# A graph attention layer: 40 instead of 32 columns per group copied by ScalarE, with one of two id loads moved ahead

## The chip, the core and the metric

The kernel runs on one core of a Trainium2 chip. The metric is the device time of one execution in microseconds; lower is better. The core has five engines with queues of their own: TensorE (PE in the profile, its weight loads PEld), VectorE (DVE), ScalarE (ACT), GpSimd (POOL) and the sync engine (SP), which issues most of the transfers. An engine's queue is handed out in order by its sequencer; instructions of the sequencer itself (loads of registers, register arithmetic) carry a q in the profile (ACTq).

## The reference

One layer of attention over a graph with N = 12500 nodes, 212500 edges sorted by target node, width 128 and 8 heads of 16. Everything is 32-bit float.

```python
Q, K, V = x @ WQ, x @ WK, x @ WV            # per node, reshaped (N, 8, 16)
Eh = edge_attr @ WE                          # per edge
score = K[src] * Q[dst] / sqrt(16) * Eh
score = exp(clip(score.sum(-1, keepdims=True), -5, 5))
wV = segment_sum(V[src] * score, dst)        # per target node
Z  = segment_sum(score, dst)
h  = x + wV / (Z + 1e-6)
h  = batchnorm(h) * gamma + beta             # over the nodes
out = layernorm(x + h)                       # over the width
```

## The kernel before

The edges lie in 1661 tiles of 128 edges. A group `g` is 8 tiles (two windows of 4), and there are 208 groups. First the kernel writes a table `kvd` of K and V for all nodes to memory (one row of 256 numbers a node). Then the main loop runs over the groups. For each tile of a group, K and V of the 128 source nodes must be brought into a slot in the on-chip memory. That is done in three ways:

- **By GpSimd.** `load_kv` appends one indirect transfer per tile (`gather`, line 272) to a list `queued`, as soon as a slot is free. A slot holds one group; the slot that `message(g)` frees is filled for group g+9. Groups 0 to 7 take another way and read no slot from `kvd`.
- **By ScalarE, as columns.** For the groups in `col_tiles` the last tile is left out of the gathers (`sizes[g] - (g in apart)`). Its 128 nodes are copied one column at a time out of `hx`, the transposed x that lies on the chip, into a tile `xc` (`fetch_cols`, line 363). Two matmuls with `w_kv` then give K and V (`cols_mm`, line 371, in the bank `ps_m`), and ScalarE copies them into the slot (`cols_out`, line 375). `COLS` is 32: 16 copies stand ahead of the exponentials of a group (`clip_exp`, lines 772 and 773) and 16 behind, so four groups make one tile. The column numbers are register values that ScalarE loads from `col_ids` (`load_cols`, line 326), in two loads of 16 words a group.
- **By the sync engine, as rows.** For the groups in `row_tiles` 16 rows a group come straight from `kvd` (`fetch_rows`, line 343), and ScalarE copies the full tile into the slot (`rows_out`, line 353).

The order on ScalarE in one group is: the first half of the column copies, the two exponentials (which wait for the scores `s` of VectorE), the second half of the copies, the writes of new x into a ring (`x_out`), `qs`, `os`, a column tile's K and V if one is due, two long copies `wt<-ps_e` (`eh_out`, line 715), the window of x for a later group (`q_window`, lines 654 and 661, `xw<-hx`; a load of 4 words from `base_i` in every second group), and the loads of the column numbers for the next group.

On VectorE a group is: `products` (line 755, which needs the gathered slot), `scores` (762), the clip (771), the work for later groups (684, 732, 809), `message` (777, which needs the exponentials) and `onehot` (674 to 677).

The order of all this is the order of the calls in the loop; nothing reorders it. From group 12 on the gathers are in addition paced: each is tied to a step of VectorE or TensorE in the loop.

Of the kernel before, what the change touches and what calls it, by code (L numbers as in the profile page):

```python
# [8 lines left out]
F32 = mybir.dt.float32  # L9
# [3 lines left out]
AF = mybir.ActivationFunctionType  # L13
OP = mybir.AluOpType
AX = mybir.AxisListType
ET = mybir.EngineType

P = 128
# [15 lines left out]
RING = 1024  # L34
MARGIN = 64
PAD = 2 * MARGIN + WN
COLS = 32
LOAD = 16
FIRST_COL = 8
COL_LAG = 2  # L40
SP_ROWS = 16
# [33 lines left out]
def col_plan(sizes):  # L75
    full = sizes.count(U) // 2
    groups, end = [], P
    while FIRST_COL + -(-end // COLS) - 1 + COL_LAG < full:
        groups.append(max(NX, FIRST_COL + -(-end // COLS) - 1 + COL_LAG))
        end += P  # L80
    assert sorted(set(groups)) == groups
    return groups


def row_plan(sizes):
    full, used = sizes.count(U) // 2, set(col_plan(sizes))
    groups, end = [], P
    while True:
        g = FIRST_ROW + -(-end // SP_ROWS) + ROW_LAG
        while g in used:  # L90
            g += 1
        if g >= full:
            return groups
        used.add(g)
        groups.append(g)
        end += P
# [7 lines left out]
def gnn_kernel(  # L104
# [19 lines left out]
    nc = tc.nc  # L124
    N, D = out.shape
# [19 lines left out]
    late = []  # L145
# [45 lines left out]
    hx = consts.tile([P, N + P], F32, name="hx")  # L191
# [66 lines left out]
    def slot(i):  # L258
        return rows.tile([P, 2 * G * P], F32, name=f"slot{i}")

    first = slot(NSLOT).rearrange("p (h c d) -> p h c d", h=2, d=2 * P)
# [34 lines left out]

    col_tiles = col_plan(usizes)
    tot = len(col_tiles) * P
    assert tot % (2 * COLS) == 0 and tot // (2 * COLS) <= P and P % COLS == COLS % LOAD == 0
    col_ids = consts.tile([P, 2 * COLS], I32, name="col_ids")  # L300
    row_tiles = row_plan(usizes)
    tot_rows = len(row_tiles) * P
# [6 lines left out]
    BY_ROW = {}  # L309
    XC = {}  # L310

    def load_col_ids():
        n, m = 2 * SP_ROWS, tot_rows // (2 * SP_ROWS)
        nc.sync.dma_start(row_ids[:m], bass.AP(tensor=rsrc.tensor, offset=rsrc.offset + tot, ap=[[n, m], [1, n]]))
        m = tot // (2 * COLS)
        nc.sync.dma_start(col_ids[:m], bass.AP(tensor=rsrc.tensor, offset=rsrc.offset, ap=[[2 * COLS, m], [1, 2 * COLS]]))

    OFFS = {}

    def load_cols(g):  # L320
        q = g - FIRST_COL
        if 0 <= q < tot // COLS:
            OFFS[g] = []
            for c in range(0, COLS, LOAD):
                at = q % 2 * COLS + c
                _, offs = nc.values_load_multi_w_load_instructions(
                    col_ids[q // 2:q // 2 + 1, at:at + LOAD], engines=(ET.Activation,), min_val=0, max_val=N - 1,
                    skip_runtime_bounds_check_because="node ids")
                OFFS[g] += offs

    def fetch_rows(g):
        q = g - FIRST_ROW
        if not 0 <= q < tot_rows // SP_ROWS:
            return
        c = q % 2 * SP_ROWS
        _, offs = nc.values_load_multi_w_load_instructions(
            row_ids[q // 2:q // 2 + 1, c:c + SP_ROWS], engines=(ET.SP,), min_val=0,
            max_val=(N - 1) * 8 * P, skip_runtime_bounds_check_because="node ids")
        for r, off in enumerate(offs, q * SP_ROWS):
            k = r // P  # L340
            if r % P == 0:
                BY_ROW[k] = late[0].tile([P, 2 * P], F32, name="byrow", bufs=2)
            d = nc.sync.dma_start(BY_ROW[k][r % P:r % P + 1, :].bitcast(U8), kvb[ds(off, 8 * P)].unsqueeze(0))
            d.then_inc(rows_in[k % NSEM], 16)
            tc.no_tile_sem_insts.add(d.ins.name)
            tc.add_to_no_dep_group(f"rows{k}", d.ins)

    def rows_out(g):
        k = (g - FIRST_ROW - ROW_LAG + 1) * SP_ROWS // P - 1
        if 0 <= k < len(row_tiles) and g == FIRST_ROW + -(-P * (k + 1) // SP_ROWS) - 1 + ROW_LAG:  # L350
# [1 line left out]
            tc.declare_fence(w.ins, group=f"rows{k}")  # L352
            step = nc.scalar.activation(KV[row_tiles[k]](G - 1, G, 0, 2 * P)[:, 0, :], BY_ROW[k], AF.Copy)
            tc.declare_no_dep(step.ins, group=f"rows{k}", reason="the semaphore of the rows")

    def fetch_cols(g, half):
        if g in OFFS:
            at = (g - FIRST_COL) * COLS
            for c in range(half * COLS // 2, (half + 1) * COLS // 2):
                k, r = col_tiles[(at + c) // P], (at + c) % P  # L360
                if r == 0:
                    XC[k] = late[0].tile([P, P], F32, name="xc", bufs=2)
                nc.scalar.activation(XC[k][:, r:r + 1], hx[:, ds(OFFS[g][c], 1)], AF.Copy)  # L363

    def col_tile(g):
        q = (g - FIRST_COL) * COLS
        return col_tiles[q // P - 1] if q > 0 and q % P == 0 and q <= tot else None

    def cols_mm(g):
        if col_tile(g) is not None:  # L370
# [62 lines left out]
    def within(f, g):  # L433
        return f(g) if 0 <= g < NG else None
# [99 lines left out]
    def load_quad(q):  # L534
        t = late[0].tile([P, RQ, U * P], U8, name="rbq", bufs=2)
        for h in (0, 1):
            nc.sync.dma_start(t[h * WN:(h + 1) * WN].rearrange("p a b -> p (a b)"), places(h, RQ * q, RQ))
        for k in range(RQ):
            RB[RQ * q + k] = t[:, k, :]
# [94 lines left out]
    def load(i):  # L634
        gs = range(2 * i, min(2 * i + 2, NG))
        if not gs:
            return
        t, n = wp.tile([P, 2, G, P], F32, name="ea", bufs=2), sum(nt(g) for g in gs)
        assert nt(2 * i) == G or len(gs) == 1
        for k, g in enumerate(gs):  # L640
            EA[g] = t[:, k]
        nc.sync.dma_start(t.rearrange("p c a b -> p (c a b)")[:, :n * P],
                          eaT[:, starts[2 * i] * P:(starts[2 * i] + n) * P])
# [249 lines left out]
    for q in range(NQ):  # L893
# [13 lines left out]
        k = q - first_step  # L907
# [64 lines left out]
    for g in range(NG - 2):  # L972
        if g % 2 == 0:
            load(g // 2 + 2)
        within(load_rel, g + 3)
        if (g + 6) % RQ == 0 and (g + 6) // RQ in quads:
            load_quad((g + 6) // RQ)
        fetch_rows(g)
        within(products, g)
        within(denom, g - 2)  # L980
        within(scores, g)
        fetch_cols(g, 0)
        within(clip_exp, g)
        within(recip, g - 2)
        within(turned_onehot, g + 2)
        within(both_halves, g + 1)
        late_x = g + 1 < nxg and g + 1 not in SLOT
        if late_x:
            turn_x(g + 1, 0, True)
            turn_x(g + 1, 4, True)  # L990
        within(add_x, g - 3)
        within(q_mm, g + 3)
        paced = g >= LATE + 4
        if not paced:
            issue()
        else:
            issue(G)
            for step in (SENT[g - 1], PARTS[g][1], PARTS[g][2], BY["both", g + 1]):
                pace(step)
        within(gather_sum, g - 1)  # L1000
        if paced:
            pace(BY["sum", g - 1])
        if not late_x:
            within(eh_mm, g + 2)
        cols_mm(g)
        fetch_cols(g, 1)
        within(x_out, g - 3)
        within(q_out, g + 3)
        within(sums_out, g - 1)
        cols_out(g)  # L1010
        rows_out(g)
        if late_x:
            project_main(g + 1)
            within(eh_mm, g + 2)
        within(eh_out, g + 2)
        within(q_window, g + 4)
        load_cols(g + 1)
        if paced:
            pace(BY["eh", min(g + 2, NG - 1)])
        within(turn_back, g + 1)  # L1020
        if paced:
            pace(BY["back", g + 1])
        within(qe_mm, g + 2)
        if paced:
            pace(BY["qe", min(g + 2, NG - 1)])
        within(attn, g - 2)
        within(message, g)
        within(onehot, g + 1)
        if g == 2:
            load_last()  # L1030
            nc.vector.tensor_scalar(row_ids, row_ids, 8 * P, None, op0=OP.mult)
        if g % (RUN // 2) == 2 and g > 2 and (g // (RUN // 2) + 1) * SEC < T:
            load_section(g // (RUN // 2) + 1)
        for i, r in enumerate(runs):
            if i and g == placed[i]:
                place(r)
        within_checks(g)
        while free and todo and todo[0] in done and not pending:
            load_x()
        bn_parts(2 * g - 5, 2 * g - 3)  # L1040
        if g == NG - 5:
            assert done >= set(range(NPRE))
            norm_first()
        if g == LATE - 1:
            tps.close()
            late.append(tps.enter_context(tc.tile_pool(name="late", bufs=1)))
        if g == LATE - 2:
            free.append(NSLOT)
            load_kv()
    last = NG - 1  # L1050
    g = last - 1
# [3 lines left out]
                           skip_runtime_bounds_check_because="a count")]  # L1055
# [332 lines left out]
```

## Time and profile before

| | us |
|---|---|
| median of 3 runs | 2059.93 (2055.01 to 2061.22) |
| the profiled execution, its own time | 2061.55 |
| its span, first to last instruction | 2059.6 |

| engine | busy us | share of the span | instructions |
|---|---|---|---|
| PE | 1768.6 | 86% | 9096 |
| DVE | 1543.5 | 75% | 3157 |
| POOL | 1541.2 | 75% | 1624 |
| ACT | 1225.2 | 59% | 8700 |

The chain that ended last lies in the last 60 us and tells nothing of the main loop. So the stage that counts must be read from the waits, the groups of instructions and the timeline. A row of a group reads: line, engine, operation, output<-inputs, shape, count | busy us, mean ns of one | idle us of the engine just before, and what ended it. A row of waits reads: who <- for whom: us in total, times, longest us. A row of the timeline reads: start us, us, engine, line, operation, names, count [idle before <- what ended it].

### The profile page before, as it was taken

Reading aid. Unit: us, or ns where it says so; the run is one execution under the profiler, and the core shown is the slowest. Engines: PE = TensorE matmul, PEld = TensorE weight load, DVE = VectorE, ACT = ScalarE, POOL = GpSimd, SP = SyncE. Lnnn points to the kernel's source line nnn. Section 1 sums busy time; section 2 is a strip of 40 time slices with the busy share of each in tenths; the row PEclk is TensorE's granted clock in tenths of the full one; section 3 lists DMA queues with packets and bytes.
Section 4 is the critical chain, followed back from the end, with each engine's and each line's share of the span. In section 5 each row is a group of like instructions: output and inputs, shape, how many; then the busy total and the mean of one; then the engine's idle time right before and its main releaser. Section 6 shows DMA issues by size and latency. Waiting matters only on the chain. (4 is left out here: it accounts for less than half of the span.)

```text
span 2059.6 us, 50464 instructions
## 1 busy us (share of the span) xinstructions
PE 1768.6 (86%) x9096; PEld 1121.2 (54%) x9096; DVE 1543.5 (75%) x3157; ACT 1225.2 (59%) x8700; POOL 1541.2 (75%) x1624
## 2 busy tenths in 40 slices
PE   7899999998888888888888888788888878888887
PEld 7676566665554545554554554454555445445556
DVE  4568899987777687777777777677777777777777
ACT  2356677766565565565665666565566566566545
POOL 7677777777777777777777777777777777777775
PEclk9999999999999999999999999999899999999998
DMA  7855556655555555555555555555555555555563
GB/s 266 304 184 180 190 186 195 203 182 188 180 167 185 174 178 175 174 188 170 175 187 166 175 190 161 181 186 175 167 184 174 170 179 184 164 179 184 192 202 127
DMA packets 133493, 379.50 MB, mean 184 GB/s; under 512 B 37631, under 2 KB 50602, under 8 KB 119338
## 3 DMA queue, kind: packets, MB, share of 16 engines
q0 software_dynamic: 75200, 204.05, 32.9%
q1 hardware_dynamic: 54776, 171.01, 23.7%
q14 instruction: 257, 2.11, 0.3%
q10 hardware_dynamic: 3186, 1.13, 0.2%
q8 instruction: 74, 1.21, 0.2%
HBM read 350.60 MB, written 25.44 MB: 183 GB/s over the span
## 5 line engine op out<-in xcount | busy, mean ns | idle before, releaser
L272 POOL DMA_INDIRECT slot<-kvd,srcs x1524 | 1451.5, 952 | 468.5 <-issue 283.5
L363 ACT ACTIVATE xc<-hx 128x1 f32 x6272 | 647.0, 190 | 267.5 <-issue 231.7
L755 DVE TENSOR_TENSOR slot<-slot,ps_t 128x512 f32<-128x512 f32 x410 | 271.4, 680 | 342.6 <-DMA slot<-kvd,srcs 254.8
L793 PE MATMUL ps_a<-msg,oh 128*128 128x136 f32 (+1 forms) x3322 | 519.6, 295 | 2.6 <-DVE msg L777 2.6
L793 PEld LDWEIGHTS ps_a<-msg,oh 128*128 128x128 f32 (+1 forms) x3322 | 419.3, 168 | 81.4 <-issue 52.2
L707 PE MATMUL ps_e<-ea,w_e 128*128 128x512 f32 x832 | 391.0, 592 | 0.1
L740 PE MATMUL ps_t<-ident,wt 128*128 128x128 f32 x1661 | 256.6, 295 | 125.0 <-DVE wt L732 121.6
L740 PEld LDWEIGHTS ps_t<-ident,wt 128*128 128x128 f32 x1661 | 197.7, 149 | 264.0 <-DVE wt L732 221.5
L777 DVE TENSOR_TENSOR msg<-slot,ps_m 128x1024 f32<-128x1024 f32 (+2 forms) x209 | 248.7, 1192 | 65.6 <-ACT slot L375 63.7
L772 ACT ACTIVATE ps_m<-s 128x64 f32<-128x64 f32 (+1 forms) x209 | 47.0, 225 | 399.1 <-DVE s L771 320.3
L732 DVE TENSOR_TENSOR wt<-wt,ps_q 128x512 f32<-128x512 f32 x416 | 264.6, 676 | 2.4 <-PE ps_q L722 2.3
L722 PE MATMUL ps_q<-ot,qs 64*128 64x512 f32 x832 | 264.3, 715 | 0.0
L762 DVE TENSOR_REDUCE s<-slot 128x64 f32<-128x1024 f32 (+1 forms) x208 | 249.8, 1202 | 0.2
L715 ACT ACTIVATE wt<-ps_e 128x512 f32<-128x512 f32 x416 | 231.9, 622 | 9.3 <-PE ps_e L707 9.1
L707 PEld LDWEIGHTS ps_e<-ea,w_e 128*128 128x128 f32 x832 | 143.5, 191 | 100.2 <-issue 98.7
L818 PEld LDWEIGHTS ps_a<-ident,at 128*128 128x128 f32 x408 | 65.9, 203 | 179.9 <-ACT xw L661 69.0
L674 DVE TENSOR_TENSOR oh<-ps_m,rel 128x512 f32<-128x512 f32 x208 | 141.7, 681 | 0.0
L694 PE MATMUL ps_a<-w_q,xw 128*128 128x128 f32 x416 | 95.6, 313 | 31.5 <-ACT xw L661 29.9
L836 ACT ACTIVATE ring<-ps_a 128x64 f32 x408 | 89.6, 220 | 46.7 <-PE ps_a L793 12.4
L818 PE MATMUL ps_a<-ident,at 128*128 128x128 f32 x408 | 106.9, 347 | 10.0 <-ACT os L798 7.0
L661 ACT ACTIVATE xw<-hx 128x64 f32 x416 | 89.1, 285 | 16.0 <-DMA hx<-xT 8.2
L371 PE MATMUL ps_m<-w_kv,xc 128*128 128x256 f32 x98 | 35.6, 447 | 71.7 <-ACT ps_m L772 71.6
(187 smaller groups left out, 1608.9 us busy)
## 6 DMA issues: line engine op xcount, KB each, us to landing
ea<-eaT SPq DMA_DIRECT2D x103, 1024.0 KB
byrow<-kvd SPq DMA_DIRECT2D x3072, 1.0 KB
slot<-kvd,srcs POOLq DMA_INDIRECT x1524
rbq<-relT SPq DMA_DIRECT2D x94, 128.0 KB
kvd<-slot SPq DMA_DIRECT2D x12, 512.0 KB
kvd<-t SPq DMA_DIRECT2D x12, 512.0 KB
ring<-xT SPq DMA_DIRECT2D x24, 256.0 KB
hT<-ring SPq DMA_DIRECT2D x23, 256.0 KB
```

The costliest lines, as they stand in the source:

```text
L272: return nc.gpsimd.indirect_dma_start(out=out, out_offset=None, in_=table, in_offset=bass.IndirectOffsetOnAxis(ap=part(SRC, e, 1), axis=0))
L363: nc.scalar.activation(XC[k][:, r:r + 1], hx[:, ds(OFFS[g][c], 1)], AF.Copy)
L707: by(("eh", g), nc.tensor.matmul(eh, w_e, EA[g][:, a:b, :].rearrange("p a b -> p (a b)"), start=True, stop=True))
L715: nc.scalar.activation(t[:, :(b - a) * P], EH[g][h], AF.Copy)
L722: by(("qe", g), nc.tensor.matmul(QE[g][h], QS[g][r], OT[g][r, :(b - a) * P], start=True, stop=True))
L732: by(("both", g), nc.vector.tensor_tensor(t, t, QE[g][h], op=OP.mult))
L740: by(("back", g), nc.tensor.transpose(ps[:, j, :], WT[g][h][:, j * P:(j + 1) * P], ident))
L755: step = nc.vector.tensor_tensor(kv, kv, PW[g][i][:, :b - a, :], op=OP.mult)
L762: step = nc.vector.tensor_reduce(SS[g][:, a:b, :], KV[g](a, b, 0).rearrange("p t (h d) -> p t h d", d=DH), axis=AX.X, op=OP.add)
L777: step = nc.vector.tensor_tensor(MSG[g][:, a:b, :P].rearrange("p t (h d) -> p t h d", d=DH), KV[g](a, b, P).rearrange("p t (h d) -> p t h ...
L793: by(("sum", g), nc.tensor.matmul(AGG[g][WN if j >= n else 0:], OH[g][j], MSG[g][:, j, :], start=(j == 0), stop=(j == n - 1)))
L818: nc.tensor.matmul(ps, AT[g], ident, start=True, stop=False)
```

## The change

`COLS` becomes 40 and `LOAD` 20. ScalarE copies 40 columns in each group, 20 ahead of the exponentials and 20 behind. A tile of 128 columns then ends within a group; `fetch_cols` finds the tile of each column, and `col_tile` tells whether one was completed in the group before. There are 61 column tiles in place of 49, beside the same 24 row tiles (61 + 24), and so 12 gathers fewer. The two loads of column numbers have 20 words each. The first now stands straight behind the two long copies of `eh_out`, ahead of `q_window`; the second stays behind `q_window`. `col_ids` is cleared by a memset and filled by two transfers, since 7808 numbers don't fill the rows of 80 evenly.

```diff
-COLS = 32
-LOAD = 16
+COLS = 40
+LOAD = 20
...
+    nc.vector.memset(col_ids, 0)
...
+        n = 2 * COLS
+        m, rest = divmod(tot, n)
+        for p, k, w in ((0, m, n), (m, 1, rest)):
+            if w and k:
+                nc.sync.dma_start(col_ids[p:p + k, :w], bass.AP(
+                    tensor=rsrc.tensor, offset=rsrc.offset + n * p, ap=[[n, k], [1, w]]))
...
-    def load_cols(g):
+    def load_cols(g, half):
         q = g - FIRST_COL
-        if 0 <= q < tot // COLS:
...
+        if 0 <= q < -(-tot // COLS):
+            at = q % 2 * COLS + half * LOAD
+            _, offs = nc.values_load_multi_w_load_instructions(
+                col_ids[q // 2:q // 2 + 1, at:at + LOAD], engines=(ET.Activation,), min_val=0, max_val=N - 1,
+                skip_runtime_bounds_check_because="node ids")
+            OFFS[g, half] = offs
+
+    def fetch_cols(g, half):
+        first = (g - FIRST_COL) * COLS + half * LOAD
+        for r, off in zip(range(first, tot), OFFS.get((g, half), ())):
+            k = col_tiles[r // P]
+            if r % P == 0:
+                XC[k] = late[0].tile([P, P], F32, name="xc", bufs=2)
+            nc.scalar.activation(XC[k][:, r % P:r % P + 1], hx[:, ds(off, 1)], AF.Copy)
+
+    def col_tile(g):
+        q = (g - FIRST_COL) * COLS
+        return col_tiles[q // P - 1] if 0 < q // P <= len(col_tiles) and q % P < COLS else None
...
         within(eh_out, g + 2)
+        load_cols(g + 1, 0)
         within(q_window, g + 4)
-        load_cols(g + 1)
+        load_cols(g + 1, 1)
```

On GpSimd, the gathers of groups 12 to 20 stand like this before; each row is one slot, and `x8` or `x7` is the number of its gathers.

```order
L272 DMA slot_897<-kvd,srcs 128x256 x8
L272 DMA slot_935<-kvd,srcs 128x256 x7
L272 DMA slot_1146<-kvd,srcs 128x256 x8
L272 DMA slot_1377<-kvd,srcs 128x256 x8
L272 DMA slot_1420<-kvd,srcs 128x256 x8
L272 DMA slot_1810<-kvd,srcs 128x256 x7
L272 DMA slot_2042<-kvd,srcs 128x256 x7
L272 DMA slot_2279<-kvd,srcs 128x256 x8
L272 DMA slot_2512<-kvd,srcs 128x256 x8
```

After, for the same groups:

```order
L272 DMA slot_898<-kvd,srcs 128x256 x8
L272 DMA slot_936<-kvd,srcs 128x256 x7
L272 DMA slot_1148<-kvd,srcs 128x256 x8
L272 DMA slot_1379<-kvd,srcs 128x256 x8
L272 DMA slot_1422<-kvd,srcs 128x256 x7
L272 DMA slot_1851<-kvd,srcs 128x256 x8
L272 DMA slot_2108<-kvd,srcs 128x256 x7
L272 DMA slot_2369<-kvd,srcs 128x256 x7
L272 DMA slot_2626<-kvd,srcs 128x256 x8
```

Before, the groups 13, 17 and 18 have seven gathers; after, 13, 16, 18 and 19. Over the whole loop column tiles stand every 3 or 4 groups instead of every 4.

On ScalarE, in the loop of group 12, from the copy `os` to the first column copy, before (ISA is the register arithmetic for a column's address):

```order
L798 ACTIVATE os<-ps_a 128x136
L375 ACTIVATE slot_935<-ps_m 128x256
L715 ACTIVATE wt<-ps_e 128x512 x2
L654 TENSOR_LOAD base_i
L661 ISA
L661 ACTIVATE xw<-hx 128x64
L661 ISA
L661 ACTIVATE xw<-hx 128x64
L326 TENSOR_LOAD col_ids x2
L363 ISA
L363 ACTIVATE xc<-hx 128x1
```

After:

```order
L802 ACTIVATE os<-ps_a 128x136
L379 ACTIVATE slot_936<-ps_m 128x256
L719 ACTIVATE wt<-ps_e 128x512 x2
L331 TENSOR_LOAD col_ids
L658 TENSOR_LOAD base_i
L665 ISA
L665 ACTIVATE xw<-hx 128x64
L665 ISA
L665 ACTIVATE xw<-hx 128x64
L331 TENSOR_LOAD col_ids
L342 ISA
L342 ACTIVATE xc<-hx 128x1
```

One of the two loads has moved ahead of the four instructions that make `xw`; the other stands where both stood. Both loads are 20 words long instead of 16.

More of the change, by code (lines that the diff above doesn't have):

```diff
@@ L298, in gnn_kernel @@
     tot = len(col_tiles) * P
-    assert tot % (2 * COLS) == 0 and tot // (2 * COLS) <= P and P % COLS == COLS % LOAD == 0
+    assert -(-tot // (2 * COLS)) <= P and COLS == 2 * LOAD
     col_ids = consts.tile([P, 2 * COLS], I32, name="col_ids")
@@ L310, in gnn_kernel @@
     XC = {}
+    nc.vector.memset(col_ids, 0)
     def load_col_ids():
+        n = 2 * COLS
[4 more added lines that the diff above has]
+                    tensor=rsrc.tensor, offset=rsrc.offset + n * p, ap=[[n, k], [1, w]]))
         n, m = 2 * SP_ROWS, tot_rows // (2 * SP_ROWS)
         nc.sync.dma_start(row_ids[:m], bass.AP(tensor=rsrc.tensor, offset=rsrc.offset + tot, ap=[[n, m], [1, n]]))
-        m = tot // (2 * COLS)
-        nc.sync.dma_start(col_ids[:m], bass.AP(tensor=rsrc.tensor, offset=rsrc.offset, ap=[[2 * COLS, m], [1, 2 * COLS]]))
     OFFS = {}
-    def load_cols(g):
+    def load_cols(g, half):
         q = g - FIRST_COL
-        if 0 <= q < tot // COLS:
[L323 to L329, printed above, removed]
+        if 0 <= q < -(-tot // COLS):
[14 more added lines that the diff above has]
+        return col_tiles[q // P - 1] if 0 < q // P <= len(col_tiles) and q % P < COLS else None
     def fetch_rows(g):
@@ L354, in rows_out @@
             tc.declare_no_dep(step.ins, group=f"rows{k}", reason="the semaphore of the rows")
[L356 to L367, printed above, removed]
     def cols_mm(g):
```

## The prediction, made before the changed kernel was run

> **What bounds the kernel now.** The chain that ended last covers only the end, so I began with the costliest groups of the page, then the timeline of POOL, then busy time by stage. First the gathers:
>
> ```profile
> L272 POOL DMA_INDIRECT slot<-kvd,srcs x1524 | 1451.5, 952 | 468.5 <-issue 283.5
> ```
>
> ```profile
> 88.43 0.94 POOL L272 DMA_INDIRECT slot<-kvd,srcs  x1 [4.37 <-issue]
> ...
> 177.95 0.95 POOL L272 DMA_INDIRECT slot<-kvd,srcs  x1 [0.31 <-issue]
> 179.20 0.94 POOL L272 DMA_INDIRECT slot<-kvd,srcs  x1 [0.30 <-issue]
> ...
> 2003.09 0.94 POOL L272 DMA_INDIRECT slot<-kvd,srcs  x1 [0.30 <-issue]
> ```
>
> A gather occupies POOL for 0.95 us, and 0.30 us pass before the next. The 1524 gathers begin at 88.43 and 2003.09, so the mean distance is 1914.66 / 1523 = 1.257 us, nearly the bare 0.95 + 0.30. POOL is "75% busy", but it stands in one unbroken row of gathers. The stages say the same (start, end, length, then busy us and count for PE, PEld, DVE, ACT and POOL, the granted clock, DMA share, GB/s):
>
> ```profile
> 100.00:400.00 300.00, 288.98 (x1590) 190.16 (x1588) 257.64 (x538) 204.92 (x1376) 227.50 (x238) 0.98 0.59 188
> 400.00:800.00 400.00, 343.27 (x1735) 210.84 (x1735) 301.17 (x612) 245.87 (x1832) 303.07 (x319) 0.94 0.57 180
> 1600.00:2000.00 400.00, 332.88 (x1702) 201.81 (x1702) 301.55 (x623) 233.26 (x1716) 303.10 (x319) 0.96 0.57 184
> ```
>
> POOL does 319 gathers in 400 us early and late (238 in 300 us at the start), while VectorE has 257.64 us of work in the first 300 us and only 301 in each 400 us later. From about 400 us on the other engines follow POOL. The waits agree:
>
> ```profile
> ACT ps_m L772 <- DVE s L771: 320.3, 133, 7.1
> DVE slot L755 <- DMA slot<-kvd,srcs: 254.8, 97, 6.6
> ACT ps_m L772 <- DVE rz L805: 76.0, 28, 5.0
> DVE msg L777 <- ACT slot L375: 63.7, 48, 5.7
> PE ps_a L694 <- ACT xw L661: 29.9, 72, 1.0
> ```
>
> VectorE waits 254.8 us for gathers, ScalarE 320.3 + 76.0 = 396.3 us for VectorE ahead of its exponentials. So GpSimd is the bound, ScalarE has slack, and how much each has must be told by the group. The `message` of three groups, 8, 45 and 207:
>
> ```profile
> 171.20 1.21 DVE L777 TENSOR_TENSOR msg<-slot,ps_m 128x1024 f32<-128x1024 f32 x1
> ...
> 462.74 1.21 DVE L777 TENSOR_TENSOR msg<-slot,ps_m 128x1024 f32<-128x1024 f32 x1
> ...
> 2009.27 0.89 DVE L777 TENSOR_TENSOR msg<-slot,ps_m 128x384 f32<-128x384 f32 x2 [0.25 <-ACT ps_m L772]
> ```
>
> At group 8 the compute is behind the gathers, and it catches up until about group 45: (462.74 - 171.20) / 37 = 7.88 us a group while it is free of POOL. Over all, (2009.27 - 171.20) / 199 = 9.24 us. So the compute could be 1.4 us a group slower before the end moved. That is the cover under which the change works.
>
> **The change part by part.** *The gain.* Twelve gathers go: 12 x 1.257 = 15.1 us, if POOL stays the bound. The bare 0.95 + 0.30 would give 15.0, so this term is narrow. The last gather would begin at 2003.09 - 15.1 = 1988.0. Behind it nothing changes: the message of group 207 starts 2009.27 - 2003.09 = 6.2 us later, and the program's end is 2061.55 - 2009.27 = 52.3 us behind that. 7808 columns at 40 a group end in group 203, as 6272 at 32 do, so no copy stands in the last groups.
>
> *More work on ScalarE.* One group there, from its exponential to the next, in the stretch in which it nowhere waits for VectorE:
>
> ```profile
> 250.99 0.21 ACT L772 ACTIVATE ps_m<-s 128x64 f32<-128x64 f32 x1
> 251.13 0.24 ACT L773 ACTIVATE msg<-s 128x64 f32<-128x64 f32 x1
> 251.28 1.57 ACT L363 ACTIVATE xc<-hx 128x1 f32 x16
> ...
> 253.54 1.12 ACT L715 ACTIVATE wt<-ps_e 128x512 f32<-128x512 f32 x2
> 254.49 0.44 ACT L661 ACTIVATE xw<-hx 128x64 f32 x2
> 256.06 1.67 ACT L363 ACTIVATE xc<-hx 128x1 f32 x16 [1.13 <-issue]
> 257.64 0.23 ACT L772 ACTIVATE ps_m<-s 128x64 f32<-128x64 f32 x1
> ```
>
> The instructions of the two loads, from the view of one line each (count, then ns least/median/most):
>
> ```profile
> L326 ACTq TENSOR_LOAD <-col_ids x392: 1006/1047/1851, 166.3 to 1967.6; - x196
> L654 ACTq TENSOR_LOAD <-base_i x104: 307/312/1286, 37.3 to 1965.6; - x104
> ```
>
> Sixteen copies stand 251.28 to 252.85, one every (1.57 - 0.19) / 15 = 0.092 us, taking 0.19 for one, or every 0.099 where the block is 1.67 long. Eight more copies are 8 x 0.097 = 0.78 us. A load of 16 words takes 1047 ns, of 4 words 312 ns: 61 ns a word. A load of 20 words is then estimated at 1.29 us, and the two cost 2 x 0.245 = 0.49 us more. Together 1.27 us a group, in 196 groups.
>
> *The load that moves.* The idle 1.13 us ahead of the copies at 256.06 is what is left of the loads. The sequencer works in order, so moving one load ahead does not shorten the sum of loads on its path; it hides only where the long copies keep the engine busy anyway, and they did that for the loads behind them too, since `xw` had already been handed over. I take nothing as a gain. What it costs: `xw` starts 253.54 + 0.95 now; behind a load of 1.29 us it starts at least 0.34 us later, and 0.3 more in every second group, where the load of `base_i` precedes it, so about 0.5 us. Its reader is the matmul L694, for which PE already waited 29.9 us in 72 groups, with the sums of the group before and the next `ps_e` queued behind it on PE. The bounds are nothing (the compute has room) and 0.5 us a group (each delay passes through).
>
> *Twelve more column tiles.* Each costs two matmuls, a copy into the slot, and the wait of `message` for that copy, 63.7 / 48 = 1.3 us on VectorE's path: 12 x 1.3 = 16 us over the loop, 0.08 us a group. *The memset* and the second transfer of ids stand once, ahead of the loop, and cost nothing where POOL is still gathering; uncovered they would be one instruction and one transfer.
>
> *What is late next.* With the gain in full the last `message` starts at 1988.0 + 6.2 = 1994.2. Group 8 starts about 0.9 us later (its loads and four more copies ahead of its exponential), at 172.1. So the compute must make 199 groups at (1994.2 - 172.1) / 199 = 9.16 us or less. Lower bound of what it will need: ScalarE's own work, 9.24 less its waits of 396.3 / 207 = 1.9, is 7.3 us a group; plus 1.27 and 0.08 it is 8.7. Upper bound: everything adds to the free rate, 7.88 + 1.27 + 0.08 = 9.23, and 9.73 with `xw`. I take 8.7, since the mean of 7.88 contains waits of ScalarE for PE and VectorE that its own longer work fills. Then the compute still catches up (POOL now needs 1512 x 1.257 / 199 = 9.55 us a group), only later than group 45, and the gain stands whole.
>
> *Slots.* POOL could stall at the start, where the compute is furthest behind. Group 17 uses the slot of group 8: free at 171.20 + 1.21 = 172.4, first gather at 177.95, so 5.5 us of room. After, that gather comes 1.25 earlier (group 16 has seven) and the slot 0.9 later: 3.4 us remain, and the room grows with each group as long as the compute is faster than POOL. Cost nothing; without that room, the shortage itself.
>
> *Skill against row.* The Trainium skill (Runtime: NRT & Kernel Launch, Instruction fetch mechanics) states about 200 ns a register for a load from main memory; by it, four more words in each of two loads would be 1.6 us in place of 0.49, an estimate, and the lower bound 9.8, past 9.16. The trace differs, 61 ns a word in loads from on-chip memory, and the measurement decides.
>
> **The sum.** 2061.55 - 15.1 = 2046.5 against the profiled execution. That one lies 1.6 us above the median of the runs, 2059.93, so against the median 2044.8; I say 2045.
>
> **The rivals.** *ScalarE becomes the bound (slower).* Place: its queue between the long copies and the exponentials, from group 8 on; it decides from 9.16 us a group, and beyond 9.24 the kernel is slower. For it speaks the upper bound of 9.23 to 9.73, against it the slack of 396.3 us. At 9.4, within these, the last message starts at 172.1 + 199 x 9.4 = 2042.7 and the time is 2095.0, against the median 2093; at 9.73 it is 2159. A load dearer by the word does the same: with 7.3 + 0.78 + 0.08 us of other work, 9.16 leaves 1.0 us for the eight words, so it decides from about 125 ns a word; the rows show 61. The Trainium skill's figure named above lies beyond that point, and the rows speak against it. Chance 0.10.
>
> *Part of the gain is lost*, by a stall for slots at the start or a compute of just over 9.16: at 9.20 the last message starts at 2002.9, 6.4 us earlier than now, and the time is 2053.5. Chance 0.07.
>
> *No change*: the removed gathers are given back, at a compute of 9.23, or POOL's distance between gathers grows. Against it: the distance is the same at 188 and at 180 GB/s. That gathers are not removed is excluded, since the order shows them gone. About 2060, chance 0.05.
>
> **How the numbers follow.** The forecast has 0.78. Its own range is 2040 to 2046: the median's term, and the runs' 2055.0 to 2061.2 less 15.1. To reach 8 in 10 I go into the partial case, up to 2053. About 0.3% (6 us) is what a measurement here can tell from no change. Faster by more: 0.78 + 0.04 of the partial case = 0.82; within 0.3%: 0.08; slower: 0.10.
>
> **What would show it.** Right: 1512 gathers still 1.257 us apart, the last at about 1988; loads of 20 words near 1.29 us; ScalarE's wait ahead of the exponentials down from 396 us to 396.3 - 196 x 1.27 = about 150; VectorE still waiting for gathers after an approach that lasts beyond group 45. Wrong: gaps of more than 0.3 us between gathers, hardly any wait of line 755 for gathers, or a message of group 207 more than 7 us behind the last gather.

## The result and the profile after

| | before | after |
|---|---|---|
| median of 5 runs, us | 2060.78 (2055.01 to 2061.9) | 2045.59 (2044.1 to 2049.78) |
| ratio, 95% interval | | 0.9934 (0.9916 to 0.9952) |
| the profiled execution, us | 2061.55 | 2049.78 |
| its span, us | 2059.6 | 2048.0 |

The kernel became faster by 15.2 us between the medians; 15.1 were forecast. The interval of the ratio stands for 10 to 17 us, so the agreement to a tenth of a microsecond is closer than these runs can tell, and that much of it is luck. The profiled execution of the changed kernel is the slowest of its five, so its trace shows less of the gain: 11.6 us between the spans. Beside the first four experiments the kernel before ran 23 times on another chip; one of these executions took 3180.64 us and is left out of the ratios given there.

The row of gathers, from the costliest groups and from the timeline of POOL:

```profile
L272 POOL DMA_INDIRECT slot<-kvd,srcs x1512 | 1441.5, 953 | 468.0 <-issue 262.5
```

```profile
90.22 0.95 POOL L272 DMA_INDIRECT slot<-kvd,srcs  x1 [4.72 <-issue]
...
1220.18 0.96 POOL L272 DMA_INDIRECT slot<-kvd,srcs  x1 [0.91 <-DVE s L766]
...
1618.58 0.95 POOL L272 DMA_INDIRECT slot<-kvd,srcs  x1 [0.31 <-issue]
1621.50 0.94 POOL L272 DMA_INDIRECT slot<-kvd,srcs  x1 [1.97 <-DVE rz L806]
...
1994.04 0.95 POOL L272 DMA_INDIRECT slot<-kvd,srcs  x1 [0.30 <-issue]
```

The 1512 gathers are (1994.04 - 90.22) / 1511 = 1.260 us apart, as the 1524 before were 1.257. The row starts 1.8 us later in this execution, and two gaps, of 0.91 us at 1220.2 and of 1.97 us at 1621.5, add 2.3; without these the last gather would stand near 1990 rather than at 1994.04, where 1988.0 was forecast. A gap of more than 0.3 us was named as a sign of a wrong forecast; the two are the only ones above 0.32 us among 1511, and the kernel before has none. The busy time is 1441.5 in place of 1451.5 us: the distance is nearly as it was, only the number fell.

What waits on the other engines:

```profile
ACT xc L342 <- issue: 231.3, 243, 1.8
DVE slot L759 <- DMA slot<-kvd,srcs: 202.5, 85, 6.4
ACT ps_m L776 <- DVE s L775: 148.7, 85, 5.3
PE ps_a L698 <- ACT xw L665: 147.5, 167, 1.7
DVE msg L781 <- ACT slot L379: 146.0, 59, 4.3
ACT xw L665 <- issue: 54.4, 128, 1.9
ACT ps_m L776 <- DVE rz L809: 33.6, 21, 5.9
```

VectorE still waits 202.5 us for gathers (254.8 before), so POOL is still the bound. The first of these waits comes at 647.6 us, ahead of group 65, in place of group 46: the compute needs longer to catch up, as was forecast.

```profile
647.60 0.69 DVE L759 TENSOR_TENSOR slot<-slot,ps_t 128x512 f32<-128x512 f32 x1 [1.70 <-DMA slot<-kvd,srcs]
```

ScalarE's wait ahead of its exponentials, its slack, fell from 396.3 to 148.7 + 33.6 = 182.3 us. Two waits grew that the change put under the cover: PE's for `xw`, 29.9 to 147.5 us, and that of `message` for a column tile's copy, 63.7 to 146.0 us.

The loads, and two groups of ScalarE in the stretch where the compute catches up:

```profile
L331 ACTq TENSOR_LOAD <-col_ids x391: 1243/1292/2037, 167.6 to 1958.1; - x196
```

```profile
258.02 1.08 ACT L719 ACTIVATE wt<-ps_e 128x512 f32<-128x512 f32 x2
259.61 0.40 ACT L665 ACTIVATE xw<-hx 128x64 f32 x2 [0.51 <-issue]
261.13 2.06 ACT L342 ACTIVATE xc<-hx 128x1 f32 x20 [1.13 <-issue]
263.33 0.23 ACT L776 ACTIVATE ps_m<-s 128x64 f32<-128x64 f32 x1
...
266.62 1.11 ACT L719 ACTIVATE wt<-ps_e 128x512 f32<-128x512 f32 x2
267.71 0.40 ACT L665 ACTIVATE xw<-hx 128x64 f32 x2
```

A load of 20 words takes 1292 ns. The window `xw` starts 1.59 us and 1.09 us behind the first long copy, in place of 0.95, and where it is late the engine stands idle for 0.51 us ahead of it; the idle time ahead of the column copies did not go (1.13 us, as before).

The messages of groups 8, 45 and 207:

```profile
172.94 1.21 DVE L781 TENSOR_TENSOR msg<-slot,ps_m 128x1024 f32<-128x1024 f32 x1
...
482.49 1.20 DVE L781 TENSOR_TENSOR msg<-slot,ps_m 128x1024 f32<-128x1024 f32 x1
...
1998.95 0.89 DVE L781 TENSOR_TENSOR msg<-slot,ps_m 128x384 f32<-128x384 f32 x2 [0.25 <-ACT ps_m L776]
```

The free compute now needs (482.49 - 172.94) / 37 = 8.37 us a group, 7.88 before: 0.49 us more, where ScalarE alone got 1.27 us. The last message stands 4.9 us behind the last gather, 6.2 before. From the last gather to the end of the span it is 54.0 us, 56.5 before; the last gather itself is only 9.0 us earlier in this execution.

### The profile page after: what moved, and what is told of

Same layout as the page of the kernel before. It is cut to its first block, busy times and chain, and to the rows that moved or that the text cites. A ratio compares the mean times of both kernels' runs of the same rounds, so it can differ in the third digit from the quotient of the medians.

```text
span 2048.0 us, 53628 instructions
## 1 busy us (share of the span) xinstructions
PE 1742.1 (85%) x9120; PEld 1104.5 (54%) x9120; DVE 1542.7 (75%) x3158; ACT 1393.5 (68%) x10248; POOL 1531.1 (75%) x1612
## 3 DMA queue, kind: packets, MB, share of 16 engines
q10 hardware_dynamic: 3186, 1.13, 0.2%
## 5 line engine op out<-in xcount | busy, mean ns | idle before, releaser
L272 POOL DMA_INDIRECT slot<-kvd,srcs x1512 | 1441.5, 953 | 468.0 <-issue 262.5
L342 ACT ACTIVATE xc<-hx 128x1 f32 x7808 | 795.7, 190 | 257.8 <-issue 231.3
L797 PEld LDWEIGHTS ps_a<-msg,oh 128*128 128x128 f32 (+1 forms) x3322 | 413.8, 166 | 79.8 <-issue 51.6
L759 DVE TENSOR_TENSOR slot<-slot,ps_t 128x512 f32<-128x512 f32 x410 | 269.3, 678 | 244.4 <-DMA slot<-kvd,srcs 202.5
L781 DVE TENSOR_TENSOR msg<-slot,ps_m 128x1024 f32<-128x1024 f32 (+2 forms) x209 | 248.5, 1191 | 154.9 <-ACT slot L379 146.0
L744 PE MATMUL ps_t<-ident,wt 128*128 128x128 f32 x1661 | 239.4, 282 | 68.6 <-DVE wt L736 64.7
L744 PEld LDWEIGHTS ps_t<-ident,wt 128*128 128x128 f32 x1661 | 187.8, 142 | 192.7 <-DVE wt L736 151.3
L726 PE MATMUL ps_q<-ot,qs 64*128 64x512 f32 x832 | 245.5, 668 | 0.0
L698 PE MATMUL ps_a<-w_q,xw 128*128 128x128 f32 x416 | 100.3, 324 | 148.1 <-ACT xw L665 147.5
L776 ACT ACTIVATE ps_m<-s 128x64 f32<-128x64 f32 (+1 forms) x209 | 46.0, 220 | 185.4 <-DVE s L775 148.7
L698 PEld LDWEIGHTS ps_a<-w_q,xw 128*128 128x128 f32 x416 | 63.6, 192 | 183.8 <-ACT xw L665 180.0
L665 ACT ACTIVATE xw<-hx 128x64 f32 x416 | 83.9, 249 | 74.4 <-issue 54.4
L822 PE MATMUL ps_a<-ident,at 128*128 128x128 f32 x408 | 103.0, 336 | 16.4 <-ACT os L802 11.6
```

The source lines that it names most:

```text
L272: return nc.gpsimd.indirect_dma_start(out=out, out_offset=None, in_=table, in_offset=bass.IndirectOffsetOnAxis(ap=part(SRC, e, 1), axis=0))
L342: nc.scalar.activation(XC[k][:, r % P:r % P + 1], hx[:, ds(off, 1)], AF.Copy)
L726: by(("qe", g), nc.tensor.matmul(QE[g][h], QS[g][r], OT[g][r, :(b - a) * P], start=True, stop=True))
L744: by(("back", g), nc.tensor.transpose(ps[:, j, :], WT[g][h][:, j * P:(j + 1) * P], ident))
L759: step = nc.vector.tensor_tensor(kv, kv, PW[g][i][:, :b - a, :], op=OP.mult)
L781: step = nc.vector.tensor_tensor(MSG[g][:, a:b, :P].rearrange("p t (h d) -> p t h d", d=DH), KV[g](a, b, P).rearrange("p t (h d) -> p t h ...
```

## The experiments

The theory: GpSimd's unbroken row of gathers sets the time, so twelve gathers fewer are the gain, ScalarE's added work is covered, and the place of the load moves nothing. The main rival: ScalarE is close to the path, and the moved load is what lets 40 columns fit.

### The load moved back

```diff
-        load_cols(g + 1, 0)
         within(q_window, g + 4)
+        load_cols(g + 1, 0)
         load_cols(g + 1, 1)
```

> 40 columns a group as in the changed kernel, but both loads of ids stand behind the window of x, as before the change. Theory (GpSimd's row of gathers is the bound, ScalarE is covered, so the place of a load moves nothing): 2045 us, within 3 us of the changed kernel, 1512 gathers 1.26 us apart; PE's wait for xw ahead of the window's matmul falls from 147 us back towards 30 us. Rival (the moved load hides under the two long copies and is what makes 40 columns fit): the compute needs about 1 us a group more, 2053 us or above, and ScalarE's wait for VectorE ahead of its exponentials nearly goes.

Measured: 2045.96 us (2043.43 to 2049.21), 0.9925 (0.9912 to 0.9939) of the kernel before: the time of the changed kernel. Its waits:

```profile
ACT xc L342 <- issue: 309.3, 245, 2.7
ACT ps_m L776 <- DVE s L775: 129.9, 75, 5.9
PE ps_a L698 <- ACT xw L665: 88.8, 149, 1.0
```

ScalarE's idle time for loads is 309.3 us in one place, where the changed kernel has 231.3 ahead of `xc` and 54.4 ahead of `xw`, 285.7 in all. The move therefore saved ScalarE 24 us, 0.1 us a group, and cost PE 147.5 - 88.8 = 59 us of waiting. Neither shows in the time. I expected PE's wait to fall to 30 us; it fell only to 88.8. The longer loads and copies raise it without the move too: to 77.9 us in the fourth run below.

### The move alone

```diff
-COLS = 40
-LOAD = 20
+COLS = 32
+LOAD = 16
```

> The changed kernel with 32 columns and loads of 16 words, 49 + 24 tiles: the move of one load alone. Theory: no gather goes, so 2060 us, within 3 us of the kernel before; PE's wait for xw rises from 30 us to over 100 us without any effect on the time. Rival (the move is a gain of its own): 2053 us or below.

Measured: 2060.61 us, 0.9994 (0.9985 to 1.0003). No change, as the theory has it. PE's wait for `xw` rose only from 29.9 to 46.3 us; my 100 was too much.

```profile
PE ps_a L698 <- ACT xw L665: 46.3, 81, 1.2
```

### Twelve gathers less, nothing more on ScalarE

Twelve gathers of the kernel before are plain transfers of the sync engine instead; they bring the first 128 rows of the table in place of the edges' rows.

```diff
+            n = sizes[g] - (g in apart)
+            for j in range(n - (g in LESS), n):
+                fills.append((NOW[0], KV[g](j, j + 1, 0, 2 * P).rearrange("p a d -> p (a d)")))
-            for j in range(sizes[g] - (g in apart)):
+            for j in range(n - (g in LESS)):
...
+            nc.sync.dma_start(fills.pop(0)[1], kvd[0:P, :])
```

> The kernel before with 12 gathers of 12 groups replaced by a plain transfer of the same 128 KB that the sync engine issues (rows 0 to 127 of the table in place of the edges' rows, so the output differs); ScalarE does nothing more. Theory: GpSimd's row is 12 gathers shorter, 15.1 us, so 2045 us. Rival (bytes or transfers bound the row, not the number of GpSimd's instructions): about 2060 us, gathers further apart than 1.257 us.

Measured: 2043.33 us, 0.9907 (0.9894 to 0.9921).

```profile
L273 POOL DMA_INDIRECT slot<-kvd,srcs x1512 | 1440.1, 952 | 465.5 <-issue 285.9
```

```profile
1988.30 0.95 POOL L273 DMA_INDIRECT slot<-kvd,srcs  x1 [0.30 <-issue]
```

The last gather stands at 1988.30, 14.8 us earlier than in the kernel before, with the same bytes moved. So the number of gathers on GpSimd sets the length of the row, not the bytes. The time fell by some 19 us; the 4 us beyond the row lie behind the last gather. From there to the end of the span it is 56.5 us in the profile of the kernel before, 52.5 here, and 54.2 and 53.6 in the second and the fourth run, where no gather went. What sets this end stays open.

### ScalarE's part alone

The kernel before, with four more copies in each half into a tile that nobody reads, and loads of 20 words.

```diff
-                    col_ids[q // 2:q // 2 + 1, at:at + LOAD], engines=(ET.Activation,), min_val=0, max_val=N - 1,
+                    col_ids[q // 2:q // 2 + 1, at:at + LOAD + MORE], engines=(ET.Activation,), min_val=0, max_val=N - 1,
...
+            for c in range(MORE):
+                nc.scalar.activation(junk[:, c:c + 1], hx[:, ds(OFFS[g][half * COLS // 2 + c], 1)], AF.Copy)
```

> The kernel before with 8 more column copies a group into a tile that nobody reads, and loads of 20 words; still 32 useful columns and 1524 gathers. It is ScalarE's part of the change without the gain: 1.27 us a group more. Theory: covered, 2060 us within 3 us of the kernel before, ScalarE's wait for VectorE ahead of its exponentials down from 396 us to about 150. Rival (ScalarE is close enough to the path that its work shows): 2066 us or above.

Measured: 2062.22 us, 0.9996 (0.9987 to 1.0006). The waits:

```profile
DVE slot L760 <- DMA slot<-kvd,srcs: 236.9, 87, 6.0
ACT ps_m L777 <- DVE s L776: 154.7, 83, 4.4
DVE msg L782 <- ACT slot L380: 100.8, 49, 4.3
PE ps_a L699 <- ACT xw L666: 77.9, 137, 1.1
ACT ps_m L777 <- DVE rz L810: 40.0, 19, 5.0
```

ScalarE's slack went from 396.3 to 154.7 + 40.0 = 194.7 us and the time stayed. Of the change, only the twelve more column tiles and the moved load are missing here. These four runs settle what the gain comes from: gain without ScalarE's work, ScalarE's work without gain, the move without either, and both without the move each came out as the theory says.

### How fast the compute is without the gathers

Two gathers of each of the groups 30 to 189 are made plain transfers in the same way (`LEAN * (30 <= g < 190)` in place of `(g in LESS)`), in the kernel before, in the changed one, and in the changed one with the load moved back. These first three and the run with 44 columns were on a chip on which the kernel before took 2792.75 us.

> The kernel before with two gathers of each of the groups 30 to 189 replaced by plain transfers of the sync engine (rows 0 to 127 of the table, so the output differs). GpSimd then needs 5.6 x 1.257 = 7.1 us a group there, so the compute is the bound and its own rate shows: theory 7.6 us a group between the messages of groups 60 and 180, total about 1750 us. Rival (the compute's own rate is near 9.2 us, the gathers only run beside it): about 2050 us.

> The same replacement in the changed kernel. Theory: the compute needs 8.4 to 8.7 us a group between the messages of groups 60 and 180, total about 1890 us, and nothing waits for gathers; the difference to the same kernel without the change is the 1.0 to 1.3 us of ScalarE's added work. Rival (the upper bound of the prediction): 9.2 us a group or more, 2000 us or above.

> The same replacement in the changed kernel with both loads behind the window of x. Theory (the moved load delays xw and hides nothing, since the sequencer goes through both loads in order): equal to the changed kernel or faster by up to 0.5 us a group, so 1810 to 1890 us. Rival (the moved load hides under the two long copies): slower by about 1 us a group, 2050 us.

Measured: 2567.26, 2558.23 and 2559.19 us. One run each. Something else bounds the kernel on that chip (last section), so they say nothing on the compute's rate. Once more, on a chip on which the kernel before took 2060.62 us:

> The kernel before with two gathers of each of the groups 30 to 189 replaced by plain transfers of the sync engine, once more, since the runs of this on another chip were slowed by something that also slowed the kernel before. GpSimd needs 7.1 us a group there. Theory: the compute's own rate is 7.5 to 7.9 us a group between the messages of groups 60 and 180, total about 1750 us. Rival (the compute's own rate is near 9.2 us): about 2050 us.

> The same replacement in the changed kernel, once more. Theory: 8.4 to 8.7 us a group between the messages of groups 60 and 180, total about 1890 us: ScalarE's added work shows once the gathers are out of the way. Rival (the upper bound of the prediction): 9.2 us a group or more, 2000 us or above; rival (ScalarE's work stays hidden behind VectorE): as the kernel before with this replacement.

> The same replacement in the changed kernel with both loads behind the window of x, once more. Theory (the moved load delays xw and hides nothing): equal to the changed kernel with the replacement, or faster by up to 0.5 us a group. Rival (the moved load hides under the two long copies): slower by 0.6 to 1.3 us a group.

Measured: 1944.82, 1966.89 and 1973.96 us, one run each. The messages of groups 60 and 180, first in the kernel before with this replacement, then in the changed kernel with it:

```profile
618.86 1.22 DVE L787 TENSOR_TENSOR msg<-slot,ps_m 128x1024 f32<-128x1024 f32 x1 [1.62 <-ACT slot L382]
...
1680.31 1.22 DVE L787 TENSOR_TENSOR msg<-slot,ps_m 128x1024 f32<-128x1024 f32 x1 [2.11 <-ACT slot L382]
```

```profile
628.41 1.22 DVE L791 TENSOR_TENSOR msg<-slot,ps_m 128x1024 f32<-128x1024 f32 x1 [3.72 <-ACT slot L386]
...
1685.80 1.21 DVE L791 TENSOR_TENSOR msg<-slot,ps_m 128x1024 f32<-128x1024 f32 x1
```

That is 8.85 and 8.81 us a group, the same with and without ScalarE's added work; I had expected 7.5 to 7.9 and 8.4 to 8.7. The replacement had made a new bound. The sync engine's wait for the buffers of the edge features, in the changed kernel and in the changed kernel with the replacement:

```profile
SPq L646 <- PE ps_e L711: 243.3, 56, 17.8
```

```profile
SPq L656 <- PE ps_e L721: 66.3, 16, 17.9
```

The sync engine hardly waits any more, with two transfers a group on top of its 16 rows. That it is late shows on ScalarE, which waits for the transfers into `ring`, first in the kernel before with the replacement, then in the changed kernel with it:

```profile
ACT ring L846 <- DMA ring<-xT: 192.7, 20, 16.6
```

```profile
ACT ring L850 <- DMA ring<-xT: 54.6, 15, 6.0
```

Without the replacement this wait is 8.1 us before and 1.2 us after the change. So the 8.85 is not the compute's own rate; the 8.81 holds much less of this wait and is nearer to it. Behind the replaced groups, from message 190 to message 203, VectorE does not wait for gathers in either trace, nor ScalarE for `ring`. First the kernel before with the replacement, then the changed one with it:

```profile
1762.93 1.21 DVE L787 TENSOR_TENSOR msg<-slot,ps_m 128x1024 f32<-128x1024 f32 x1
...
1865.09 1.21 DVE L787 TENSOR_TENSOR msg<-slot,ps_m 128x1024 f32<-128x1024 f32 x1
```

```profile
1772.17 1.22 DVE L791 TENSOR_TENSOR msg<-slot,ps_m 128x1024 f32<-128x1024 f32 x1
...
1888.27 1.21 DVE L791 TENSOR_TENSOR msg<-slot,ps_m 128x1024 f32<-128x1024 f32 x1
```

That is 7.86 and 8.93 us a group: here 1.07 of ScalarE's added 1.27 us shows. Most of the 22 us between these two runs arises here too, since the changed kernel is 5.5 us behind at message 180 and 23.9 us at the last. It is a stretch of 13 groups in one execution of each. With all of the change, then, the compute makes 8.4 to 8.9 us a group, below the 9.16 it needs, but not far below.

With the load moved back the rates are 8.82 between messages 60 and 180 and 8.86 between 190 and 203, within 0.1 us of the changed kernel's. The 7 us by which that single run was slower fit neither the theory nor the rival; 5.8 of them are there at message 60.

### 44 columns

> 44 columns a group and loads of 22 words, 67 + 24 tiles, 1506 gathers. GpSimd's row is 7.5 us shorter than in the changed kernel (2038 us), and the compute needs 0.64 us a group more: 8.4 to 8.7 plus 0.68 is 9.1 to 9.4, where (1994.2 - 7.5 - 172) / 199 = 9.12 is the most that keeps the gain. Theory: at the edge, 2038 to 2050 us. Rival (ScalarE still far from the path): 2038 us with VectorE waiting for gathers as much as in the changed kernel.

```diff
-COLS = 40
-LOAD = 20
+COLS = 44
+LOAD = 22
```

Measured: 3214.61 us, 1.1505 (1.1432 to 1.1578) of the kernel before on the same slow chip. Far outside what either theory gave. It shows in the loads:

```profile
L331 ACTq TENSOR_LOAD <-col_ids x390: 16/2650/5107, 248.7 to 3117.8; - x195
```

```profile
1504.48 1.12 ACT L719 ACTIVATE wt<-ps_e 128x512 f32<-128x512 f32 x2
1506.29 0.40 ACT L665 ACTIVATE xw<-hx 128x64 f32 x2 [0.69 <-issue]
1511.36 2.25 ACT L342 ACTIVATE xc<-hx 128x1 f32 x22 [4.67 <-issue]
```

Loads of 22 words took a median of 2650 and up to 5107 ns, where 61 ns a word would give 1.41 us; ScalarE stands idle for 4.67 us behind the second here, and for 1148.0 us ahead of column copies in all, where the changed kernel with the replacement has 505.3 on the same chip. On the same chip the changed kernel's loads of 20 words (with the two gathers replaced) kept near 1.29 us, so on that chip this belongs to the kernel. Why, was not tried, nor was 44 columns run on another chip.

### More rows by the sync engine

```diff
-SP_ROWS = 16
+SP_ROWS = 20
```

> The changed kernel with 20 instead of 16 rows a group by the sync engine: 61 + 30 tiles, 1506 gathers, nothing more on ScalarE but six copies of a row tile. Theory: six gathers fewer are 7.5 us, 2038 us, as long as the sync engine, which gets about 1.6 us a group more to issue and load, keeps the transfers of the edge features in time. Rival (the sync engine becomes the bound): 2050 us or above, and matmuls that wait for the edge features.

Measured: 2038.74 us (2034.91 to 2040.23), 0.9895 (0.9879 to 0.9912). It is the fastest version here: 6.9 us below the changed kernel's median, or 5.5 us if each is taken against the runs of the kernel before beside it, where six gathers are 7.5.

```profile
L272 POOL DMA_INDIRECT slot<-kvd,srcs x1506 | 1433.1, 952 | 465.6 <-issue 274.0
```

```profile
DVE msg L781 <- ACT slot L379: 284.0, 61, 11.1
ACT ring L840 <- DMA ring<-xT: 125.5, 23, 11.1
ACT ps_m L776 <- DVE s L775: 43.8, 36, 4.4
```

```profile
SPq L646 <- PE ps_e L711: 57.2, 12, 17.9
```

```profile
231.44 0.94 POOL L272 DMA_INDIRECT slot<-kvd,srcs  x1 [0.90 <-PE ps_a L797]
```

The cover is used up here: the sync engine's wait is 57.2 us (243.3 in the changed kernel), ScalarE's for VectorE 43.8, and VectorE nowhere waits for a gather any more. `message` waits 284.0 us for column tiles; their copies stand behind the writes into `ring`, for whose transfers ScalarE now waits 125.5 us (1.2 in the changed kernel). So it is the sync engine that is late here, with four rows a group more, while ScalarE got only six copies of a row tile more. GpSimd's row has four gaps of 0.49 to 0.98 us near its start, 2.0 us beyond the usual 0.30 in all; the one shown is the first. That the next gather taken off would bring less than its 1.26 us is likely, but was not run.

## Why the prediction was right, point by point

- **The gain**, 12 x 1.257 = 15.1 us: the medians differ by 15.2, and the distance of the gathers stayed within 0.003 us. The third experiment shows the gain without the change's other parts: its last gather is 14.8 us earlier. That nothing would change behind the last gather did not hold to the microsecond: in the changed kernel's profile this end is 2.5 us shorter, and the row ends 6 us later than forecast. The two partly cancel. In the first experiment's profile the row ends at 1988.2 us, as forecast for the changed kernel.
- **The loads**, 1.29 us from the two rows of 16 and 4 words: 1.292. The slack should have fallen to about 150 us and fell to 182.3; it lost 214 us, not 249. In the fourth experiment, where the row of gathers kept its length, the added work took 202 us of it.
- **The moved load**, no gain and up to 0.5 us a group: PE's wait for `xw` rose by 117.6 us, 0.6 us a group. The experiments split it: 16 us from the move alone, 48 from the longer work alone, the rest from both and the twelve more tiles together. The 0.1 us a group that it saved on ScalarE was not foreseen.
- **Column tiles**, 1.3 us each on VectorE's path: mis-sized. The wait rose by 82 us, not by 16, to 2.5 us each. The copy into the slot stands behind the second half of the column copies, and the fourth experiment, with the same 49 tiles and the longer work, has 100.8 us of it, 2.1 us each: the work made every tile dearer, old and new. Twelve more tiles at that price are 25 us; the remaining 20 stay open.
- **The compute's need**, taken as 8.7 of at most 9.16 us a group: 8.37 in the free stretch, 8.81 under the replacement and 8.93 behind it. The reason given, that longer work fills ScalarE's waits, fits the early stretch, where 0.49 of its 1.27 us showed, and hardly the late one, where 1.07 did. There the rate lies about midway between 8.7 and the upper bound of 9.23, which adds everything up. What sets the two stretches apart was not looked into.
- **The rivals**: ScalarE as the bound is refuted by the fourth experiment, the moved load as the cause by the first two. TensorE's granted clock was higher after the change, 0.976 against 0.951, but the third experiment has the gain at 0.945. The forecast was nearer to the edge than it looked: about 0.2 us a group were left late in the loop, and four rows more used the cover up. The run with four columns more failed by its loads, on another chip, and does not show where ScalarE's own edge lies.

## What to carry to other kernels

An engine that is busy 75% of the span can still be the bound: look whether its instructions follow one another at a constant distance from the first to the last, and price the change by that distance. Then ask what the other engines have as cover by the group, and compare it with what the change adds; a load that is moved ahead in an engine's own queue may save next to nothing, as the 0.1 us a group here. When an experiment takes the bound away, look which engine has stopped waiting before you call the new rate that of the one you meant, and look for a stretch behind the replacement where neither bound is left.

## What was not expected of the hardware

A load of register values cost 61 ns a word from 4 to 20 words (312, 1047 and 1292 ns), but with two loads of 22 words a group, on the one chip where that was run, it took 2650 ns in the median and up to 5107 ns; on that chip loads of 20 words kept a median of 1291 ns.

One chip ran the kernel before in 2792.75 us, where the others took about 2060. There the register arithmetic ahead of a column copy took up to 1413 ns in the changed kernel with the replacement, at the same median of 37 ns; the first row is from that chip, the second from the other:

```profile
L349 ACTq FUSED_REGOPS  x7808: 3/37/1413, 251.4 to 2476.8; - x196
```

```profile
L349 ACTq FUSED_REGOPS  x7808: 37/37/37, 169.9 to 1885.2; - x196
```

So single instructions of ScalarE's sequencer took far longer there. What held them up, and whether that makes the whole difference, the traces don't show.
